# An earlier start for each scan direction's preparation, and a skewed first norm, in a four-layer vision-scan kernel

## The chip, the cores and the metric

The kernel runs on one core of a Trainium2 chip, in float32 throughout. The metric is device time in microseconds (us) for the whole program. Five engines work side by side, each through its own list of instructions in a fixed order: TensorE (PE, matrix products into PSUM), VectorE (DVE), ScalarE (ACT), GpSimd (POOL) and SyncE (SP), which here only issues data transfers (DMAs).

## The reference

Four layers follow each other on an image of shape (4, 96, 64, 64). Layers 0 and 2 are two-layer selective scans with a batch norm at the end, layer 3 is a depthwise 7x7 convolution with an MLP. The change is in layer 1, a state-space model in its chunked form (SSD), applied along four directions of each image:

```python
xn = rmsnorm(x, norm_w)                       # over the 96 channels
xs = [xn, flip(xn), transpose(xn), flip(transpose(xn))]   # 4 directions, 4096 tokens each
z, xBC, dt = split(xs @ in_proj_w.T)          # 192 | 192+128+128 | 3 heads
dt  = softplus(dt + dt_bias)
xBC = silu(conv_b + causal_conv4(xBC))
xh, Bm, Cm = split(xBC);  A = -exp(A_log)
# in chunks of tokens, with dAc = cumsum(dt * A):
y  = (Cm Bm^T * exp(dAc_s - dAc_t) * dt) @ xh + exp(dAc) * (Cm @ state)
y  = (y + D * xh) * silu(z)
y  = rmsnorm(y, gnorm_w) @ out_proj_w.T
out = mean over the 4 directions, each put back in place, + x
```

`x` of layer 1 is the result of layer 0: its batch norm's scale and shift applied to the raw output, plus layer 0's input.

## The kernel before

`program` (L1223) runs `mamba_fusion` (layer 0), `ssd` (layer 1), `mamba_fusion` (layer 2) and `convnext` (layer 3) one after the other. `mamba_fusion` leaves its output un-normed in DRAM (`raw`) and hands on scale and shift (`norm`); the next block applies them as it loads.

**How SSD is tiled.** A chunk is Q = 128 tokens, a block BLK = 1024 tokens or eight chunks. `run` (L986) lists 64 steps (b, o, r, blk): batch b of 4, orientation o (0 as it is, 1 transposed), r (0 forwards, 1 backwards), and 4 blocks. So 16 steps make a batch, and every fourth step begins a direction. The 512 chunks go through one loop with lags: `sums_to` (loads `dr`), `decay` (`seg`), `weights` (`cb`, `seg`, `xs`), `outputs` (`y`, state `prev`, `yz`, and at L931 its square sum on ACT), `scale`, `by_channels`, `finish` (adds into `X`, an SBUF image of the batch).

**The front of a block** (L780) is made while the block before it is worked on: `z` (PE L796, for r = 0 only), the two halves of the convolution (PE L814 and L825 from the stacked shifted copies `pk`), their additions (ACT L819, DVE L830), the silu (ACT L112) and transposes (L842). It is a generator, of which each point of the loop takes one step (two for the first block of an orientation), and it is finished at the block's last chunk.

**The preparation of a direction** is `prelude` (L763), also a generator. For r = 0 and o = 0 it begins with `rmsnorm` (L666): for each of NT = 8 pieces of 512 tokens, load `raw` and the residual, apply scale and shift (ACT L673), add (DVE L674), write the sum to DRAM (`src`), square (ACT L677), mean over channels (PE L679), inverse root (ACT L107, twice), and the product into `xn[0]` (DVE L682). For o = 1 it begins with `turn` (L685), eight transposing copies on POOL. Then `step_sizes` (L696): eight rows of dt (PE L706, ACT L711, a DMA to DRAM, L712), one load in another layout (`dtx`, L717), a softplus (L719 on), a transpose (L725). Last come `decays` (L729): PE L743, L745, L756, and a DMA of `rows`, from which `dr` is loaded. For r = 1 only `decays` is left. The loop takes one step of the preparation per chunk, and the rest at once at a fixed chunk:

```python
if n >= 0 and preludes and n // QB >= preludes[0][0] - 3:
    if n == (preludes[0][0] - 1) * QB - 1:
        for _ in preludes.pop(0)[1]:
            pass
```

So for a direction whose first step is N, the steps begin with block N - 3 and the rest is taken at the last chunk of block N - 2, before the front of step N begins.

**Start of SSD.** Two pieces of the norm, then all weights (`weights_of`, L616), then the rest of the first preparation, then `switch(0)` (L975: `X` loaded from `src`), then the whole first front, then the loop.

**What sets the order.** The code issues operations in program order; a scheduler then places them on the engines, and moves an operation ahead where its operands and buffers are free. Buffers come from pools, and a tile's buffer is taken over in program order: the tag "front" has two PSUM banks, which the preparation's products share with the fronts. All DMAs are issued by SP. Each transfer has one of a few semaphores in turn, and waits until the transfer that had it last is done.

Of the kernel before, what the change touches and what calls it, by code (L numbers as in the profile page):

```python
# [18 lines left out]
F32 = mybir.dt.float32  # L19
AF = mybir.ActivationFunctionType  # L20
ALU = mybir.AluOpType
# [4 lines left out]
B, C, HH, WW = 4, 96, 64, 64  # L26
# [546 lines left out]
class Ssd:  # L573
# [42 lines left out]
    def weights_of(self, w):  # L616

        nc, k, one = self.nc, self.k, self.one
        self.inw = one.tile([C + 1, 2 * DI + 2 * DST + NH], F32, name="inw")
        nc.sync.dma_start(self.inw, w["in"])  # L620

        conv = self.work.tile([P, 3 * BLK], F32, tag="pk", name="conv")
        conv = conv[:C, : 4 * CONV].rearrange("c (k n) -> c k n", k=4)
        nc.sync.dma_start(conv, w["conv_wT"].partition_broadcast(C))
        xbc = self.inw[:C, DI : DI + CONV]
        nc.vector.tensor_tensor(conv, conv, xbc[:, None].to_broadcast([C, 4, CONV]), ALU.mult)
# [12 lines left out]
        self.a = one.tile([P, 1, NH], F32, name="a")  # L639
        k.act.exp_ln(self.a[:, 0], self.ad[:, 0], AF.Exp)  # L640
        nc.vector.tensor_scalar_mul(self.a, self.a, -1.0)

        self.opw = one.tile([P, 4, C], F32, name="opw")
        gn = one.tile([P, 4], F32, name="gn")
        nc.vector.memset(self.opw, 0.0)
        nc.vector.memset(gn, 0.0)  # L650
        low, up = slice(0, HD), slice(HD, P)
        for j, rows, n, of in (
            (0, slice(0, P), slice(0, P), 0), (1, low, low, 1), (2, up, low, 0), (3, low, up, 0),
            (3, up, up, 2),
        ):
            nc.sync.dma_start(self.opw[rows, j], w["out"][n, of])
            nc.sync.dma_start(gn[rows, j : j + 1], w["gnorm"][n, of : of + 1])
        for j in range(4):
            nc.vector.tensor_scalar(
                self.opw[:, j], self.opw[:, j], gn[:, j : j + 1], 0.25, ALU.mult, ALU.mult  # L660
            )

    def bank(self, tag):
        return self.psum.tile([P, T], F32, tag=tag, name=tag, bufs=2)

    def rmsnorm(self, b):  # L666
        nc, k = self.nc, self.k
        for c in range(NT):
            t = ds(c * T, T)
            x, res = (self.work.tile([C, T], F32, name=n) for n in ("nx", "nr"))  # L670
            nc.sync.dma_start(x, self.raw[b, :, t])
            nc.sync.dma_start(res, self.res[b, :, t])
            nc.scalar.activation(x, x, AF.Identity, bias=self.bn[1], scale=self.bn[0])  # L673
            nc.vector.tensor_tensor(x, x, res, ALU.add)  # L674
            nc.sync.dma_start(self.src[b, :, t], x)
            sq = self.work.tile([C, T], F32, name="nsq")
            nc.scalar.activation(sq, x, AF.Square)  # L677
            pv = self.bank("front")[:C]
            nc.tensor.matmul(pv, lhsT=k.mean, rhs=sq, start=True, stop=True)  # L679
            rsqrt(k.act, sq, pv, self.eps)  # L680
            xn = self.xn[0][:C, ds(PAD + c * T, T)]
            nc.vector.scalar_tensor_tensor(xn, x, self.norm, sq, ALU.mult, ALU.mult)  # L682
            yield

    def turn(self):  # L685
# [7 lines left out]
            )  # L693
            yield

    def step_sizes(self, o):  # L696

        nc, k = self.nc, self.k
        n = NQ * NH
        rows = self.dram.tile([NH, L], F32, name="dtrows")
        for c in range(NT):
            pd = self.bank("front")[:NH]
            nc.tensor.matmul(  # L706
                pd, lhsT=self.inw[:, DI + CONV :], rhs=self.xn[o][:, ds(PAD + c * T, T)],
                start=True, stop=True,
            )
            row = self.work.tile([C, T], F32, tag="nsq", name="dtrow")[:NH]  # L710
            nc.scalar.copy(row, pd)  # L711
            nc.sync.dma_start(rows[:, ds(c * T, T)], row)  # L712
            yield
        x, ua, lg = (
            self.work.tile([n, Q], F32, tag=m, name=m, bufs=1) for m in ("dtx", "ua", "row")
        )
        nc.sync.dma_start(x, rows.rearrange("h (c t) -> c h t", t=Q))  # L717
        yield
        nc.scalar.activation(ua, x, AF.Abs)  # L719
# [43 lines left out]
    def prelude(self, b, o, r):  # L763

        if r == 0:
            yield from self.rmsnorm(b) if o == 0 else self.turn()
            yield from self.step_sizes(o)
        self.seq[b, o, r] = self.decays(r)

    def stack(self, o, r, blk):  # L770
# [9 lines left out]
    def front(self, b, o, r, blk, made, following):  # L780
# [205 lines left out]
    def run(self):  # L986
# [16 lines left out]
        def front(n):  # L1003
            if n >= len(steps):
                return iter(())
            return self.front(*steps[n], made[n], steps[n + 1] if n + 1 < len(steps) else None)
# [3 lines left out]
            (n, self.prelude(*steps[n][:3])) for n in range(0, len(steps), nblk)  # L1010
        ]
        first = preludes.pop(0)[1]
        for _ in range(2):
            next(first)
        self.weights_of(self.w)
        for _ in first:
            pass
        self.switch(0)
        for _ in front(0):
            pass  # L1020
        for n in range(-4, len(chunks) + 4):
            def at(lag):
# [289 lines left out]
```

## Time and profile before

| | us |
|---|---|
| median of 8 runs | 10003.18 (9988.59 to 10021.0) |
| profiled execution, own time | 10021.0 |
| its span, first to last instruction | 10019.0 |
| busy PE / DVE / POOL / ACT | 8622.6 / 8167.7 / 6975.5 / 5529.7 |
| norm's scale of layer 0 ready (end of DVE L561) | 3075 |
| first and last chunk's square sum (ACT L931) | 3191.8 and 6251.8 |
| moved by DMA | 1528.27 MB |

In the profile, busy time is that of executing instructions; PEld is the load of weights into PE, and lies beside PE's products. A row of the timeline gives the start, the length, the engine, the line, what is written from what, how many instructions were merged, and in brackets how long the engine had been idle and which engine or DMA ended that. SPq is SP's queue. The granted clock is that of PE, 1 being full speed.

### The profile page before, as it was taken

Reading aid. Unit: us, or ns where it says so; the run is one execution under the profiler, and the core shown is the slowest. Engines: PE = TensorE matmul, PEld = TensorE weight load, DVE = VectorE, ACT = ScalarE, POOL = GpSimd, SP = SyncE. Lnnn points to the kernel's source line nnn. Section 1 sums busy time; section 2 is a strip of 40 time slices with the busy share of each in tenths; the row PEclk is TensorE's granted clock in tenths of the full one; section 3 lists DMA queues with packets and bytes.
Section 4 is the critical chain, followed back from the end, with each engine's and each line's share of the span. In section 5 each row is a group of like instructions: output and inputs, shape, how many; then the busy total and the mean of one; then the engine's idle time right before and its main releaser. Section 6 shows DMA issues by size and latency. Waiting matters only on the chain. (4 is left out here: it accounts for less than half of the span.)

```text
span 10019.0 us, 109739 instructions
## 1 busy us (share of the span) xinstructions
PE 8622.6 (86%) x32744; PEld 3567.1 (36%) x32744; DVE 8167.7 (82%) x10861; ACT 5529.7 (55%) x10500; POOL 6975.5 (70%) x4600
## 2 busy tenths in 40 slices
PE   7888888888886988988898888788888888888688
PEld 1222222222213676676776777122221122221122
DVE  7999999999984666666766667799999999999787
ACT  5566666656653445545545544566666665665244
POOL 6888888888884555555555555688888888888322
PEclk9999999999987999999999999899999999998798
DMA  7677777667763223222322221767777777776442
GB/s 191 199 206 205 201 204 206 197 196 209 202 196 113 70 68 92 70 64 82 87 62 73 86 64 50 190 198 205 206 200 206 207 203 199 207 203 198 112 100 73
DMA packets 803534, 1528.27 MB, mean 153 GB/s; under 512 B 124253, under 2 KB 128249, under 8 KB 802170
## 3 DMA queue, kind: packets, MB, share of 16 engines
q1 hardware_dynamic: 802938, 1521.25, 53.6%
q8 instruction: 260, 4.26, 0.2%
q14 instruction: 336, 2.75, 0.1%
HBM read 1229.69 MB, written 156.37 MB: 138 GB/s over the span
## 5 line engine op out<-in xcount | busy, mean ns | idle before, releaser
L342 POOL TENSOR_TENSOR hc<-hs,bc 128x1024 f32<-128x1024 f32 x1536 | 3610.7, 2357 | 648.1 <-DVE hs L340 577.5
L340 DVE TENSOR_TENSOR_SCAN hs<-da,carry,bs 128x512 f32<-128x512 f32 x2016 | 2466.8, 1265 | 79.7 <-DVE bs L335 1.9
L107 ACT ACTIVATE da<-da,w_a 128x512 f32<-128x512 f32 x2304 | 1614.5, 715 | 1244.1 <-DMA da<-dd 1193.8
L361 PE MATMUL py<-hc,selsum 128*32 128x512 f32 x6144 | 1806.1, 640 | 469.6 <-POOL hc L342 459.3
L313 PE MATMUL bs<-du,seldu 64*128 64x512 f32 x4608 | 1589.0, 682 | 205.4 <-DVE hs L340 191.7
L335 DVE TENSOR_TENSOR bs<-bs,bc 128x1024 f32<-128x1024 f32 x1152 | 1398.5, 1214 | 196.8 <-PE bs L313 193.1
L308 POOL TENSOR_TENSOR du<-du,bc 128x1024 f32<-128x1024 f32 x384 | 905.1, 2357 | 273.1 <-DMA du<-dg 166.7
L361 PEld LDWEIGHTS py<-hc,selsum 128*32 128x32 f32 x6144 | 239.1, 110 | 1816.0 <-POOL hc L342 1113.5
L313 PEld LDWEIGHTS bs<-du,seldu 64*128 64x128 f32 x4608 | 451.7, 197 | 1208.2 <-DVE hs L340 850.1
L879 POOL TENSOR_TENSOR seg<-seg,cb 128x384 f32<-128x384 f32 x512 | 515.5, 1008 | 509.4 <-DVE cb L878 389.4
L194 PE MATMUL pu<-h,w_conv 96*128 96x512 f32 (+3 forms) x2048 | 832.7, 627 | 6.0 <-ACT rs L107 6.0
L863 DVE TENSOR_SCALAR seg<-dr,dac 128x128 f32<-128x128 f32 x1536 | 620.3, 436 | 261.5 <-PE y L908 244.5
L340 DVE TENSOR_TENSOR_SCAN hs<-bs,carry,du 128x512 f32<-128x512 f32 x672 | 823.5, 1260 | 6.5 <-issue 4.5
L814 PE MATMUL front<-pk,sconv 128*128 128x512 f32 x1536 | 746.3, 605 | 10.8 <-ACT z L802 7.0
L883 POOL TENSOR_TENSOR xs<-pre,coef 128x576 f32<-128x576 f32 x512 | 598.2, 1174 | 204.3 <-PE halves L922 148.6
L918 POOL TENSOR_TENSOR y<-y,xs 128x192 f32<-128x192 f32 x496 | 294.5, 594 | 545.5 <-DVE y L917 542.9
L931 ACT ACTIVATE y<-yz 128x192 f32<-128x192 f32 x512 | 186.1, 363 | 862.8 <-DVE yz L930 861.9
L825 PE MATMUL front<-sconv,pk 128*128 128x192 f32 x3072 | 572.8, 330 | 51.6 <-DVE pre L830 44.2
L1175 DVE SCALAR_TENSOR_TENSOR acc<-pad,c_conv,acc 96x1024 f32<-96x1024 f32 x336 | 491.5, 1467 | 110.2 <-ACT acc L1166 58.9
L345 ACT COPY carry<-hs 128x2 f32<-128x2 f32 x1344 | 251.1, 187 | 575.6 <-DVE hs L340 571.9
L825 PEld LDWEIGHTS front<-sconv,pk 128*128 128x128 f32 x3072 | 497.7, 190 | 82.4 <-DVE pre L830 70.2
L107 ACT ACTIVATE bs<-da,w_a 128x512 f32<-128x512 f32 x768 | 522.1, 680 | 3.4 <-DVE hs L340 1.4
(196 smaller groups left out, 13974.0 us busy)
## 6 DMA issues: line engine op xcount, KB each, us to landing
da<-dd SPq DMA_DIRECT2D x3072, 256.0 KB
du<-dg SPq DMA_DIRECT2D x768, 256.0 KB
dr<-rows SPq DMA_DIRECT2D x256, 384.0 KB
bc<-rows SPq DMA_DIRECT2D x256, 256.0 KB
dd<-delta SPq DMA_DIRECT2D x192, 256.0 KB
dg<-du SPq DMA_DIRECT2D x192, 256.0 KB
pk<-xn SPq DMA_DIRECT2D x128, 384.0 KB
pk<-xn SPq DMA_DIRECT2D x128, 256.0 KB
```

Of the source, the lines that this page charges most:

```text
L107: self.last = self.scalar.activation(out, in_, func, **kw)
L194: nc.tensor.matmul(pu[r0:r1], lhsT=wt["conv"][:kk, tap, d0:d1], rhs=h[:kk, b, ds(tap, T)], start=(tap == 0), stop=(tap == 3),)
L308: nc.gpsimd.tensor_tensor(g["du"], g["du"], self.b_or_c(g, 0), ALU.mult)
L313: nc.tensor.matmul(g["bs"][:, i], lhsT=self.sel["du"][rows, g["half"], g["q"]], rhs=g["made"]["du"][rows, g["j"]], start=True, stop=True,)
L335: nc.vector.tensor_tensor(dbx, dbx, self.b_or_c(g, 0), ALU.mult)
L340: nc.vector.tensor_tensor_scan(hs[:, i], da[:, i], dbx[:, i], init, ALU.mult, ALU.add)
L342: nc.gpsimd.tensor_tensor(g["hc"], hs, self.b_or_c(g, 1), ALU.mult)
L361: nc.tensor.matmul(py[rows], lhsT=self.sel["sum"][:, g["q"]], rhs=g["hc"][:, i], start=(g["q"] == 0), stop=(g["q"] == NQU - 1),)
L814: nc.tensor.matmul(p, lhsT=self.conv[:, i, DI + q * DST : DI + (q + 1) * DST], rhs=pk[:, i, ds(c * T, T)], start=(i == 0), stop=(i == 2),)
L825: nc.tensor.matmul(p, lhsT=pk[:, i, ds(c * Q, Q)], rhs=self.conv[:, i, :DI], start=(i == 0), stop=(i == 2),)
L863: nc.vector.tensor_scalar(seg[:, h], g["pair"]["dr"][:, c % 2 * NH + h], made["dac"][:, n0 + h : n0 + h + 1], 0.0, ALU.subtract, ALU.min,)
L883: nc.gpsimd.tensor_tensor(xs, x.to_broadcast([P, 3, NH, HD]), coef.to_broadcast([P, 3, NH, HD]), ALU.mult)
```

## The change

Three things are edited.

1. In the loop the preparation's steps begin one block earlier (`- 4` for `- 3`).
2. The first batch's norm is a new function, `begin`. All pieces are loaded at once, `raw` into `X` and the residual into `xn[1]`; the sum stays in `X`, so neither `src` nor the reload is needed for batch 0. The pieces go through in stages of which each is one piece behind the one before it, down to the dt rows. The weights are loaded in three parts, by a generator, and the first front is issued in between the steps of the preparation (one step after every third of the front).
3. In `rmsnorm` of the other batches each piece is loaded one step ahead of its use, which makes nine steps of eight. The write to `src`, and the dt rows' write to DRAM for all directions, are issued from ACT's queue instead of SP's.

```diff
@@ weights_of
         nc.sync.dma_start(conv, w["conv_wT"].partition_broadcast(C))
+        yield
         xbc = self.inw[:C, DI : DI + CONV]
...
         nc.vector.tensor_scalar_mul(self.a, self.a, -1.0)
+        yield
...
+    def begin(self):
+        nc, k = self.nc, self.k
+        rest = self.xn[1][:C]
+        for c in range(NT):
+            nc.sync.dma_start(self.X[:, ds(c * T, T)], self.raw[0, :, ds(c * T, T)])
+            nc.sync.dma_start(rest[:, ds(PAD + c * T, T)], self.res[0, :, ds(c * T, T)])
+            if c == 1:
+                yield
+        self.batch = 0
+        rows = self.dram.tile([NH, L], F32, name="dtrows")
+        sq, pd = {}, {}
+        for n in range(NT + 4):
+            if 0 <= (c := n - 4):
+                row = self.work.tile([C, T], F32, tag="nsq", name="dtrow")[:NH]
+                nc.scalar.copy(row, pd.pop(c))
+                nc.scalar.dma_start(rows[:, ds(c * T, T)], row)
+            if n < NT:
+                x = self.X[:, ds(n * T, T)]
+                nc.scalar.activation(x, x, AF.Identity, bias=self.bn[1], scale=self.bn[0])
+                nc.vector.tensor_tensor(x, x, rest[:, ds(PAD + n * T, T)], ALU.add)
+                sq[n] = self.work.tile([C, T], F32, tag=("nx", "nr")[n % 2], name="sq")
+                nc.scalar.activation(sq[n], x, AF.Square)
+            if 0 <= (c := n - 1) < NT:
+                pv = self.bank("front")[:C]
+                nc.tensor.matmul(pv, lhsT=k.mean, rhs=sq[c], start=True, stop=True)
+                rsqrt(k.act, sq[c], pv, self.eps)
+            if 0 <= (c := n - 2) < NT:
+                xn = self.xn[0][:C, ds(PAD + c * T, T)]
+                nc.vector.scalar_tensor_tensor(
+                    xn, self.X[:, ds(c * T, T)], self.norm, sq.pop(c), ALU.mult, ALU.mult
+                )
+            if 0 <= (c := n - 3) < NT:
+                pd[c] = self.step_rows(0, c)
+        return rows
+
     def rmsnorm(self, b):
...
+        loaded = []
+        for c in range(NT + 1):
+            if loaded:
+                n, x, res = loaded.pop()
+                nc.scalar.activation(x, x, AF.Identity, bias=self.bn[1], scale=self.bn[0])
+                nc.vector.tensor_tensor(x, x, res, ALU.add)
+                sq = self.work.tile([C, T], F32, name="nsq")
+                nc.scalar.activation(sq, x, AF.Square)
+                nc.scalar.dma_start(self.src[b, :, ds(n * T, T)], x)
...
+            if c < NT:
+                x, res = (self.work.tile([C, T], F32, name=n) for n in ("nx", "nr"))
+                nc.sync.dma_start(x, self.raw[b, :, ds(c * T, T)])
+                nc.sync.dma_start(res, self.res[b, :, ds(c * T, T)])
+                loaded.append((c, x, res))
             yield
...
+    def step_rows(self, o, c):
+        pd = self.bank("front")[:NH]
+        self.nc.tensor.matmul(
+            pd, lhsT=self.inw[:, DI + CONV :], rhs=self.xn[o][:, ds(PAD + c * T, T)],
+            start=True, stop=True,
+        )
+        return pd
+
-    def step_sizes(self, o):
+    def step_sizes(self, o, rows=None):
...
-            nc.scalar.copy(row, pd)
-            nc.sync.dma_start(rows[:, ds(c * T, T)], row)
-            yield
+        if rows is None:
+            rows = self.dram.tile([NH, L], F32, name="dtrows")
+            for c in range(NT):
+                row = self.work.tile([C, T], F32, tag="nsq", name="dtrow")[:NH]
+                nc.scalar.copy(row, self.step_rows(o, c))
+                nc.scalar.dma_start(rows[:, ds(c * T, T)], row)
+                yield
...
     def prelude(self, b, o, r):
         if r == 0:
-            yield from self.rmsnorm(b) if o == 0 else self.turn()
-            yield from self.step_sizes(o)
+            if (b, o) == (0, 0):
+                rows = yield from self.begin()
+                yield
+            else:
+                rows = None
+                yield from self.rmsnorm(b) if o == 0 else self.turn()
+            yield from self.step_sizes(o, rows)
         self.seq[b, o, r] = self.decays(r)
...
     def front(self, b, o, r, blk, made, following):
-        made.update(self.seq[b, o, r])
+        made.update(self.seq.get((b, o, r), {}))
...
     def run(self):
-        for _ in range(2):
-            next(first)
-        self.weights_of(self.w)
+        weights = self.weights_of(self.w)
+        next(first)
+        next(weights)
+        next(first)
+        next(weights)
+        for m, _ in enumerate(front(0)):
+            if m % 3 == 2:
+                next(first, None)
         for _ in first:
             pass
-        self.switch(0)
-        for _ in front(0):
+        made[0].update(self.seq[steps[0][:3]])
+        for _ in weights:
             pass
...
-            if n >= 0 and preludes and n // QB >= preludes[0][0] - 3:
+            if n >= 0 and preludes and n // QB >= preludes[0][0] - 4:
```

More of the change, by code (lines that the diff above doesn't have):

```diff
@@ L666, in rmsnorm @@
     def rmsnorm(self, b):
         nc, k = self.nc, self.k
[L668 to L682, printed above, removed]
+        loaded = []
@@ new lines, in rmsnorm @@
+        for c in range(NT + 1):
[6 more added lines that the diff above has]
+                nc.scalar.dma_start(self.src[b, :, ds(n * T, T)], x)
+                pv = self.bank("front")[:C]
+                nc.tensor.matmul(pv, lhsT=k.mean, rhs=sq, start=True, stop=True)
+                rsqrt(k.act, sq, pv, self.eps)
+                xn = self.xn[0][:C, ds(PAD + n * T, T)]
+                nc.vector.scalar_tensor_tensor(xn, x, self.norm, sq, ALU.mult, ALU.mult)
+            if c < NT:
[3 more added lines that the diff above has]
+                loaded.append((c, x, res))
@@ L694, in turn @@
             yield
-    def step_sizes(self, o):
+    def step_rows(self, o, c):
[6 more added lines that the diff above has]
+    def step_sizes(self, o, rows=None):
         nc, k = self.nc, self.k
         n = NQ * NH
[L703 to L710, printed above, removed]
-            nc.scalar.copy(row, pd)
-            nc.sync.dma_start(rows[:, ds(c * T, T)], row)
-            yield
+        if rows is None:
[5 more added lines that the diff above has]
+                yield
         x, ua, lg = (
```

## The prediction

> **What bounds the kernel now.** I read the page first, for which engine leads and where.
>
> ```profile
> span 10019.0 us, 109739 instructions
> PE 8622.6 (86%) x32744; PEld 3567.1 (36%) x32744; DVE 8167.7 (82%) x10861; ACT 5529.7 (55%) x10500; POOL 6975.5 (70%) x4600
> ```
>
> The change touches only the SSD stage, so everything is read there. It runs from 3075 us (the batch norm's scale is done at 3074.96) to 6257 us (last addition to X, L973). The 512 instructions of ACT L931, eight to a block of 1024 tokens, date its 64 blocks: the first at 3191.8, the last at 6251.8. So 116.8 us pass before the first, and the blocks take the rest. Their lengths from that list: 42 to 48 us for most, but four blocks before each new image orientation are long. For batch 0, blocks 4 to 7 take 44.0, 44.2, 54.9 and 57.5 (200.6 us); blocks 12 to 15, ahead of the next batch, 44.8, 56.9, 56.3 and 57.7 (215.7).
>
> Then the busy time by window: the start-up, blocks 4 to 7, and block 8 (columns: length, PE, PEld, DVE, ACT, POOL, granted clock, DMA share, GB/s).
>
> ```profile
> 3075.00:3192.00 117.00, 58.68 (x168) 29.68 (x168) 28.39 (x74) 45.25 (x71) 24.09 (x22) 0.67 0.50 146
> 3373.00:3416.00 43.00, 39.11 (x221) 31.31 (x220) 30.62 (x78) 21.27 (x50) 24.91 (x31) 0.96 0.25 74
> 3416.00:3461.00 45.00, 40.70 (x218) 31.29 (x218) 32.42 (x83) 21.20 (x51) 26.25 (x33) 0.92 0.25 71
> 3461.00:3516.00 55.00, 50.60 (x252) 34.98 (x252) 30.83 (x81) 24.80 (x57) 27.76 (x34) 0.91 0.16 46
> 3516.00:3573.00 57.00, 48.94 (x240) 40.19 (x240) 27.18 (x84) 26.97 (x62) 23.45 (x29) 0.85 0.21 64
> 3573.00:3621.00 48.00, 42.39 (x240) 34.30 (x239) 34.41 (x93) 24.43 (x59) 27.81 (x35) 0.96 0.25 75
> ```
>
> In a plain block PE is busy nine tenths: PE is the bound, and added PE work costs its length. The start-up is different, with no engine above 50%: a chain of waits. Block 7 has 8.1 us of idle PE and a clock of 0.85.
>
> The timeline shows why. First the start-up:
>
> ```profile
> 3095.31 2.02 DVE L626 TENSOR_TENSOR conv<-conv,inw 96x1792 f32<-96x1792 f32 x1 [9.17 <-DMA conv<-in_L_conv_wT]
> 3105.73 0.53 SPq L671 DMA_DIRECT2D nx<-raw  x1
> 3108.76 0.81 ACT L673 ACTIVATE nx<-nx,bn 96x512 f32<-96x512 f32 x1 [12.16 <-DMA nx<-raw]
> 3147.20 0.58 SPq L717 DMA_DIRECT2D dtx<-dtrows  x1
> 3149.78 0.31 ACT L719 ACTIVATE ua<-dtx 96x128 f32<-96x128 f32 x1 [4.20 <-DMA dtx<-dtrows]
> ```
>
> SP sits behind the weights' copies, so the third of eight pieces is loaded 30 us after the first. Then block 7:
>
> ```profile
> 3508.71 0.57 SPq L717 DMA_DIRECT2D dtx<-dtrows  x1
> 3518.39 0.29 ACT L719 ACTIVATE ua<-dtx 96x128 f32<-96x128 f32 x1
> 3528.33 3.04 PE L796 MATMUL front<-inw,xn 96*128 96x192 f32 x16
> 3531.29 10.57 PE L814 MATMUL front<-pk,sconv 128*128 128x512 f32 x24
> 3541.70 8.03 PE L825 MATMUL front<-sconv,pk 128*128 128x192 f32 x48
> 3554.74 1.09 PE L842 MATMUL front<-ident,pre 128*128 128x128 f32 x8 [2.98 <-ACT pre L112]
> ```
>
> The preparation is flushed at the end of block 6. Its last products hold the two "front" banks until 3527, so the whole front of block 8 comes in one lump of 21.4 us late in block 7, with PE waiting around it (ACT's silu).
>
> **What the Trainium skill says.** "DMA: Bandwidth & Descriptors", Anatomy of one DMA: a transfer has a fixed cost near 2.0 us besides its bytes. Here dtx, 48 KB, is read 2.6 us after its issue: agrees. The same page, Issuing engines are not separate DMA queues: another issuing engine saves only sequencer time. No run so far shows a DMA issued from ACT; SP's x<-nx issues take 0.30 us, dtrows 0.26. "Perfetto Trace Analysis", DMA Instruction HWDGE: the issuing sequencer itself waits for the semaphores before it is free; SP's queue above behaves so. "TensorE: Matmul & The Clock Gate", What's actually happening: idle stretches halve the array's clock. The 0.85 of block 7 and the 0.67 of the start-up agree.
>
> **The change part by part.** In the order in which the built instructions stand on each engine: before, the first orientation change has its decays at chunk 60 and the next front wholly behind them at chunk 61. After, the decays stand at chunk 50 and that front is spread over chunks 55 to 59. So the change does what it says.
>
> *Start-up.* Twelve transfers go (eight copies of x, four reloads of X: 3 MB); the sixteen piece loads are issued at once, ahead of the weights' dependent copies. Step by step, as estimates from the rows:
> - 18 issues of about 0.43 us from 3075.8. Their bytes (16 x 192 KB, inw 244 KB, conv 672 KB) are 4.1 MB; at 206 GB/s, the page's busy slices, 19.8 us, so the last lands near 3097. DVE's product of conv waits for 1.7 MB, 8.4 us and 2 us fixed, ends near 3088.5, and holds the third piece until then.
> - ACT per piece: 0.81 + 0.63 + 0.68 + 0.63 + 0.57 (row copy) + 0.30 (issue) = 3.6 us, eight times 29 us, 5.5 of it done by 3088. So 3112, and 3 us for the skewed stages: 3115 (3145 before).
> - Row landing to dtx read, 4.2 us before: 3119. Softplus to decays, 5.9 before, plus 3 between the front's groups: 3128. Decay rows to the first seg, 8.4 before: 3136.5.
> - The front meanwhile: z 4.9, conv 10.6 plus 2.1 of decays, to 3132. Its last 8.0 us need DVE's additions, which stand behind seg: to 3144.
> - Ahead of the silu ACT has the next batch's first piece, whose load SP issues behind six dr loads, and a copy out of it that waits for DVE. Behind these are the silu, hence PE's transposes and all chunks. I take 5 us: 3149. Silu to first L931, 12.4 before: 3162, against 3191.8. Gain 30 us. Bounds: 15 (DMA or the 5 us twice as bad) to 42 (no such holds).
>
> *Orientation changes* (four). Block 4 stays 44.0: the eight POOL copies lie under PE. The eight rows, 10.7 us over a plain block, move from block 6 to 5: 54.9. Block 6 keeps 44.2 plus the decays' PE work (0.42 + 0.58 + 0.69 + 0.42 = 2.1) and 1 us of wait: 47.3. Block 7 becomes a block that makes a front with z, 46.7 (mean of blocks 8 to 10), plus 1.7 for the reverse direction's decays: 48.4. Sum 194.6, against 200.6: 6 us, in all 24. Bounds for all: 0 to 30.
>
> *Batch changes* (three). Sums before 215.7, 216.7, 219.1: mean 217.2. After: block 12 takes the eight norms (12.5), 57; block 13 the rows in the tangle that block 14 shows now, 55; block 14 keeps two rows (2.7), decays (2.1), and 3 for its last conv products, which stand in one lump behind the decays: 52; block 15 48.4. Sum 212.4: 4.8 us, in all 14. Bounds: -10 (the norm, a block earlier, disturbs more) to 33 (all stalls gone: 206 each).
>
> *Copies moved to ACT.* Of 88 issues, 80 are in the steady part: 0.3 us each, 24 us of ACT. I cost them at nothing: ACT is busy 21 to 27 us of each 44 to 57. Without that cover they cost 24. Each also waits until an earlier transfer that used its semaphore has landed; behind it on ACT stand the exponentials of seg and the evacuations of front banks, for which POOL and PE wait. Before, these waits were SP's, which fed only loads issued early. Eight transfers stand between, usually over 10 us of this stage, so I take 0.
>
> Sum: 30 + 24 + 14 = 68 us. Against the profiled execution (10021 us, span 10019) that gives 9953. That execution was the slowest of the eight; against their median, 10003, it gives 9935.
>
> **Rivals.**
> 1. Only the start-up gains. PE is the bound in every block, and every product of the preparation remains, only elsewhere; the rows' 10.7 us speak for it. Against it: block 7's 8.1 us of idle PE and low clock. 10003 - 30 = 9973.
> 2. All stalls go. Start-up 40, orientation changes to plain work (three blocks of 44.2, one of 46.7, rows 10.7, decays 3: 193, thus 30 in all), batch changes to 206 (12.5 more for the norm; 33 in all): 9900. Against it: the lumps that remain in blocks 13 and 14 of the new order.
> 3. Slower: ACT becomes the place where DMA waits are served. If each of the 80 issues holds ACT, and PE behind it, for t, the gain is gone at 68/80 = 0.85 us, and it is slower beyond 0.2% at 1.1 us. At 2 us it gives 10003 - 68 + 160 = 10095. For it: ACT's order is fixed, and an SP load it waits for can itself be late (dr waits up to 15 us). Against: the distance of eight transfers, and ACT's idle half.
>
> **How the numbers follow.** Likeliest case 0.60 (own range 9915 to 9955); only the start-up 0.17; all stalls 0.13; slower 0.07; gains and losses cancelling 0.03. Predicted 9935. The range, 9890 to 9985, takes in the second and third case with their bounds and leaves out the slow one and most of the cancelling one. About 0.2%, 20 us, is what a measurement of this kernel can tell from no change. Faster by more: 0.60 + 0.13 + 0.15 of the start-up case = 0.88. Within: 0.05. Slower: 0.07.
>
> **What would show it.** First L931 near 3162 (the stage's start being the same); blocks 7, 23, 39 and 55 near 48 us with a clock over 0.9 and no 21 us lump; blocks 5 and its like near 55; block 12 near 57. Wrong would be: ACT idle for DMA ahead of its row copies or x copies, blocks 5 or 12 above 60, or a silu of the first front that waits long for nx.

## The result

The changed kernel takes 9935.5 us (median of 11 runs, 9914.2 to 9946.0) beside 10009.4 for the kernel before in the same comparison: a ratio of 0.9929, 95% interval 0.9919 to 0.9940, so about 71 us less. All differences below are worked out in this way: the ratio's distance from one, times the median of the kernel before that ran beside it.

The first lines of the page of the kernel after, span and busy time by engine:

```profile
span 9936.8 us, 109594 instructions
PE 8582.2 (86%) x32744; PEld 3521.3 (35%) x32744; DVE 8210.0 (83%) x10861; ACT 5529.3 (56%) x10500; POOL 6977.6 (70%) x4600
```

PE has the same 32744 products and is busy 40 us less. The change took no product from it; the same products last less, in line with a mean granted clock over the execution of 0.935 beside 0.930.

The stage's start (end of DVE L561) is at 3059.4 us here, against 3075.1 before; layer 0 is untouched, and over all executions below this lies between 3054 and 3087. So all places in the stage are counted from that point. L931 of before is L985 now. The busy time by window, for the start-up and then blocks 4 to 8 (columns: length, PE, PEld, DVE, ACT, POOL, clock, DMA share, GB/s):

```profile
3059.00:3157.00 98.00, 67.26 (x175) 31.33 (x175) 29.21 (x79) 43.90 (x73) 24.69 (x23) 0.64 0.48 138
3337.00:3380.00 43.00, 39.42 (x217) 31.57 (x216) 30.36 (x79) 20.77 (x50) 24.43 (x30) 0.92 0.24 74
3380.00:3435.00 55.00, 51.49 (x244) 33.49 (x243) 33.35 (x84) 25.11 (x58) 27.31 (x35) 0.94 0.21 60
3435.00:3483.00 48.00, 42.61 (x239) 34.92 (x237) 34.41 (x90) 24.92 (x63) 27.16 (x35) 0.93 0.22 68
3483.00:3527.00 44.00, 37.82 (x224) 30.64 (x224) 26.49 (x73) 22.96 (x54) 22.01 (x27) 1.00 0.22 64
3527.00:3576.00 49.00, 44.49 (x252) 36.31 (x250) 34.92 (x95) 24.98 (x57) 28.15 (x35) 0.97 0.24 73
```

Block 7 is now 44 us at a clock of 1.00 (57 at 0.85 before). The orientation's dt rows, now made in block 5, make that block ten us longer (53.9 on average beside 43.9). In sum over the stage, from the list of all 512 instructions of that line, the profiled executions differ so:

| part of the SSD stage | before | after | difference | prediction |
|---|---|---|---|---|
| start to the first L931/L985 | 116.7 | 97.4 | -19.3 | -30 |
| blocks 4 to 7 of each batch (4 groups) | 798.1 | 759.0 | -39.1 | -24 |
| blocks 12 to 15 (3 groups) | 651.4 | 638.7 | -12.7 | -14 |
| all other blocks | 1610.5 | 1603.9 | -6.6 | 0 |
| stage | 3176.7 | 3099.0 | -77.7 | -68 |

The time came out as forecast, but two of the four terms did not: the start-up gave a third less, the orientation changes 15 us more. The timeline of the new start-up shows the first:

```profile
3062.13 0.42 SPq L624 DMA_DIRECT2D conv<-in_L_conv_wT  x1
3069.97 1.02 SPq L675 DMA_DIRECT2D xn<-in_x  x1
3077.33 0.31 SPq L674 DMA_DIRECT2D X<-raw  x1
3079.06 2.02 DVE L627 TENSOR_TENSOR conv<-conv,inw 96x1792 f32<-96x1792 f32 x1 [9.45 <-DMA conv<-in_L_conv_wT]
3079.55 0.81 ACT L688 ACTIVATE X<-X,bn 96x512 f32<-96x512 f32 x1 [9.37 <-DMA X<-raw]
3113.97 0.58 SPq L766 DMA_DIRECT2D dtx<-dtrows  x1
3120.72 0.30 ACT L768 ACTIVATE ua<-dtx 96x128 f32<-96x128 f32 x1
```

The third piece reaches ACT 20.1 us after the stage's start, not 13.4, and dtx is used 6.75 us after its load's issue. And block 6, with the decays, and the front of block 8 in block 7, on PE:

```profile
3446.51 0.27 PE L805 MATMUL front<-ident,dac 128*96 128x128 f32 x1
...
3480.60 2.74 PE L868 MATMUL front<-pk,sconv 128*128 128x512 f32 x6
3484.04 2.84 PE L868 MATMUL front<-pk,sconv 128*128 128x512 f32 x6 [0.70 <-ACT z L856]
3488.04 1.88 PE L868 MATMUL front<-pk,sconv 128*128 128x512 f32 x4
```

The decays are through 36 us before block 7 begins (3482.8), and the front is cut into small portions with chunks between.

### The profile page after: what moved, and what is told of

Read it like the earlier page. It is cut to its first block, busy times and chain, and to the rows that moved or that the text cites. A ratio compares the mean times of both kernels' runs of the same rounds, so it can differ in the third digit from the quotient of the medians.

```text
span 9936.8 us, 109594 instructions
## 1 busy us (share of the span) xinstructions
PE 8582.2 (86%) x32744; PEld 3521.3 (35%) x32744; DVE 8210.0 (83%) x10861; ACT 5529.3 (56%) x10500; POOL 6977.6 (70%) x4600
## 5 line engine op out<-in xcount | busy, mean ns | idle before, releaser
L985 ACT ACTIVATE y<-yz 128x192 f32<-128x192 f32 x512 | 186.1, 363 | 907.8 <-DVE yz L984 907.0
L1235 DVE SCALAR_TENSOR_TENSOR acc<-pad,c_conv,acc 96x1024 f32<-96x1024 f32 x336 | 491.9, 1468 | 110.8 <-ACT acc L1226 59.9
```

Source lines behind the costliest of these rows:

```text
L1235: nc.vector.scalar_tensor_tensor(acc, images[b % 2][:, y : y + rows, x : x + WW], wt["conv"][:, tap : tap + 1], acc, ALU.mult, ALU.add,)
```

## The experiments

Where a kernel is called "early" or "late", that is when a preparation begins: with the first block of the direction ahead (as changed) or the second (as before). The flush is the rest of a preparation, taken at once at its fixed chunk. The orientation groups are blocks 4 to 7 of each batch, the batch groups blocks 12 to 15 of the first three. Sums of the stage's parts are from one profiled execution each. Groups of 16 blocks that no edit touches (blocks 0 to 3, and 8 to 11, of all four batches) lie between 721 and 737 us in all these executions, so a sum's difference under some 16 us says little by itself.

### Which part carries the gain

One edit to the kernel before:

```diff
-            if n >= 0 and preludes and n // QB >= preludes[0][0] - 3:
+            if n >= 0 and preludes and n // QB >= preludes[0][0] - 4:
```

> The kernel before with one edit: a preparation begins a block earlier. The start-up, the order inside the norm and the queue of the small copies stay as they were. By the prediction's steps: 24 us at the orientation changes and 14 at the batch changes, so 38 us below the kernel before. By the comparison of the two traces (39 us at the orientation changes, 13 at the batch changes, some 7 in the other blocks): 52 to 58 below. The rival in which only the start-up gains: no difference from before. First L931 of the stage at the same distance from the stage's start as before, about 117 us.

Measured: ratio 0.9926 (0.9909 to 0.9942), 74 us less. The start-up stays at 118.2 us; the orientation groups fall by 52 us to 745.9, the batch groups by 16 to 635.7. The rival in which only the start-up gains falls. But this one line alone gives as much as the whole change, so the rest of the change is worth nothing net, or parts of it cancel.

The reverse edit, made to the changed kernel (`- 4` back to `- 3`):

> The changed kernel with one edit undone: a preparation begins as late as before. What is left of the change is the new start-up, the norm in two skewed halves and the small copies on ACT's queue. By the prediction's steps: 30 us below the kernel before. By the comparison of the two traces: 19 to 25 below. The rival in which only the start-up gains: all of the 71 us. The long blocks ahead of an orientation change (blocks 7, 23, 39, 55) come back near 57 us, with their 21 us lump of the next block's front.

Measured: ratio 1.0016 (1.0006 to 1.0027), 16 us *more* than before, which no theory had. The start-up gained its 19.2 us, but the orientation groups are 9 us longer than before and the batch groups 23 us longer. So something in the rest of the change costs, more so when the beginning is late. Two candidates: the copies on ACT's queue and the skewed norm. The next run takes the first away, by giving the three `nc.scalar.dma_start` of small copies back to `nc.sync`:

> The run with the late beginning again (preparations as late as before, new start-up, skewed norm), but with the small copies back on SP's queue. With the copies on ACT that run was 19 us above the kernel before, its start-up 19 us shorter and its blocks 31 us longer. If the copies on ACT's queue are what lengthens the blocks, this run is 20 to 30 us below the kernel before, with the orientation and batch changes as before within 10 us. If it is the skewed norm, it stays within 10 us of the kernel before and the blocks ahead of a batch change stay 20 us longer in sum.

Measured: ratio 1.0003 (0.9996 to 1.0011), no difference that can be measured; start-up 91.9 us. The orientation groups come back to 793.4 (798.1 before), so there it was the copies, as far as so small a sum tells. The batch groups do not: 681.7, 30 us above before. There it is the norm's skew, the one thing left that touches them. The next two runs show by what means.

### What makes block 7 long

The prediction read from the trace that the late decays keep the two front banks and force the next front into one lump, and that the lump costs. This kernel is the changed one with the tail of each preparation left for the flush. The norm's nine steps and the eight rows (17), or the eight of the turn and the eight rows (16), are still taken one to a chunk:

```diff
-                else:
+                elif (steps[preludes[0][0]][2] == 0
+                      and n - (preludes[0][0] - 4) * QB < (17 if steps[preludes[0][0]][1] == 0 else 16)):
                     next(preludes[0][1], None)
```

> The changed kernel, in which each later preparation still starts a block earlier, but only its norm or turn and its rows are made early: the softplus, the decays and what follows wait until the last chunk of the block before last, where the kernel before made them. Theory: the late decays hold the two front banks and push the next block's front into a lump in block 7, and the 39 us at the orientation changes come from taking the decays away from there. Then blocks 7, 23, 39 and 55 go back to 55 to 58 us from 44.5, the preparations lose 10 us each, and of the 71 us some 15 to 35 are left. Rival: the gain comes from spreading the rows and the turn thinner; then the time is that of the changed kernel within 15 us.

Measured: ratio 0.9925 (0.9908 to 0.9943), 75 us less: nothing lost. In this kernel dtx's load and the first exponentials still come early, 48 and 43 us ahead of block 7; the decays come right at its start (3485.4). PE's timeline, with the decays' last product first:

```profile
3484.87 0.27 PE L805 MATMUL front<-ident,dac 128*96 128x128 f32 x1
...
3485.75 2.30 PE L850 MATMUL front<-inw,xn 96*128 96x192 f32 x12
...
3488.79 10.46 PE L868 MATMUL front<-pk,sconv 128*128 128x512 f32 x24
...
3502.03 6.01 PE L879 MATMUL front<-sconv,pk 128*128 128x192 f32 x36
```

The lump is there, 22 us of front with hardly a chunk between, as in the kernel before. But it begins with the block and not 13 us into it, and the block takes 45.0 us. So the lump by itself costs nothing; its lateness does.

Then it should not matter when a preparation begins, only when it ends. The kernel before with one edit:

```diff
                 else:
-                    next(preludes[0][1], None)
+                    for _ in range(2):
+                        next(preludes[0][1], None)
```

> The kernel before with one edit: a preparation still begins with the second block of the direction ahead, but takes two of its steps a chunk in place of one, so that it is through as early as in the changed kernel. Theory: block 7 is long because the chain of rows, dtx, softplus and decays ends some 13 us into it and the next front can't begin before; then only the end of the preparation counts, blocks 7, 15 and their like go to 45 to 47 us, and most of the gain is there, 45 to 75 us below the kernel before. Rival: beginning a block earlier gains because the preparation's work is spread thinner; then doubling it up in block 5 (13) costs what block 7 saves, and the time is within 20 us of the kernel before.

Measured: ratio 0.9928 (0.9913 to 0.9942), 72 us less, with a late beginning and the old start-up. Blocks 7 and 15 take 44.6 and 44.3 us on average. So what counts is when the preparation ends. The doubling up is not free before an orientation: block 6 takes 52.4 us there against 46.9 with the early beginning, and the orientation groups 770 us against 746. Before a batch it is better than free: 587 us against 636.

Over these runs the relation can be read off: the place of the decays' transposition on PE (L756, L805 in the changed kernel), from the block's start, against the length of that block (7, 15, 23, 31, 39, 47 and 55).

| kernel | decays, us from the block's start | length of the block, us |
|---|---|---|
| two steps a chunk, late | -40 to -35 | 44.3 to 45.4 |
| changed kernel | -37 to -31 | 44.5 to 45.5 |
| tail at the last chunk | -0.5 to 0.1 | 45.0 to 46.1 |
| before | 11.1 to 11.8 | 57.5 to 59.6 |
| late, skewed norm, copies on ACT | 13.6 to 14.6 | 59.9 to 61.0 |
| late, skewed norm, copies on SP: before an orientation | 11.0 to 11.7 | 57.8 to 59.2 |
| the same: before a batch | 16.0 to 16.3 | 63.8 to 64.4 |

From zero on, the block lasts the decays' delay and 45.5 to 48.3 us more: that is the time from the decays over the front to the next block's first sum. Before zero, being earlier buys one or two microseconds at most. This also explains the two runs with the late beginning. The skewed norm takes nine steps where the old one takes eight, so one more row waits for the flush; with the copies on SP the decays then come 4 to 5 us later, with those on ACT 2 us. Before an orientation the copies on ACT bring the decays to 14.4 us, from 11.1.

### The copies on ACT's queue

The changed kernel with L685, L716 and L761 issued by SP (`nc.scalar.dma_start` back to `nc.sync.dma_start`, three places):

> The changed kernel with the 88 copies that it gave to ACT's queue (L685, L716, L761) issued by SP again. The prediction costs the move at nothing: the same time as the changed kernel, within 10 us, so 61 to 81 below the kernel before. If the issues on ACT (0.24 to 0.50 us each in the changed kernel's trace, 80 in the steady part) lay on the path, 24 us would come back: 95 below. If instead it was the move that gave room to SP's loads, the gain shrinks to 50 or less, and SP's waits ahead of dr, nx and nr grow.

Measured: ratio 0.9891 (0.9875 to 0.9906), 109 us less than before and 38 less than the changed kernel; the two intervals lie apart. In the stage itself the two profiled executions differ by 20.6 us; the rest lies in layers that the edit doesn't touch. So I put the cost at 20 to 38 us, 0.23 to 0.43 us for each of the 88 copies. The prediction costed it at nothing. In the two kernels with the late beginning the same move is worth less: 1.0016 against 1.0003 is 13 us with intervals that overlap, and the stage differs by 5.5 us (start-up and orientation groups 19 us less on SP, batch groups 8 more).

Which blocks have it can be told over several runs. The start-up takes 97.1 to 97.5 us in the three runs with the copies on ACT and 91.9 to 94.3 in seven with them on SP. A part of that can be followed, in the changed kernel:

```profile
3141.47 0.81 ACT L712 ACTIVATE nx<-nx,bn 96x512 f32<-96x512 f32 x1 [8.08 <-DMA nx<-raw]
3142.31 0.69 DVE L713 TENSOR_TENSOR nx<-nx,nr 96x512 f32<-96x512 f32 x1 [2.36 <-ACT nx L712]
3142.92 0.35 DVE L884 TENSOR_TENSOR pre<-front,xbias 128x192 f32<-128x192 f32 x1
```

ACT waits 8.1 us for the next batch's first piece, DVE waits for ACT, and the front's last addition (L884) stands behind both. It begins 3.3 us after the addition before it, where the earlier ones are 1.0 us apart, and the silu needs it. With the copies on SP this piece comes to ACT at 3165.00, after the first L985 (3160.24): the edit changed the order that is built, and not only who issues. That is 2.4 us of about 5.

Block 12, with the norm's copies of x, takes 58.5 and 58.6 us on average in two runs with them on ACT and 54.0 to 54.9 in three with them on SP: about 12 us for three batches. Block 5, with the rows' copies, takes 53.7 and 53.9 us beside 51.8 to 53.7, which is hardly apart. In the three blocks 12 PE stands 10.3 us on average in the changed kernel and 8.3 with the copies on SP, and its products take 48.2 us beside 46.6, at a clock of 0.91 beside 0.93. A place where the two kernels differ, first in the changed one:

```profile
3749.78 0.88 PE L976 MATMUL halves<-xs,bt 128*128 128x192 f32 x2 [2.52 <-DVE cb L932]
3750.45 1.91 PE L718 MATMUL front<-nsq,mean 96*96 96x512 f32 x2
3752.16 1.38 PE L962 MATMUL y<-xs,seg 128*128 128x64 f32 x6
...
3764.67 1.05 PE L718 MATMUL front<-nsq,mean 96*96 96x512 f32 x2
```

And at the same place with the copies on SP:

```profile
3746.51 0.59 PE L976 MATMUL halves<-xs,bt 128*128 128x192 f32 x2 [1.27 <-DVE cb L932]
3746.93 1.02 PE L718 MATMUL front<-nsq,mean 96*96 96x512 f32 x2
3748.29 1.15 PE L962 MATMUL y<-xs,seg 128*128 128x64 f32 x6 [0.33 <-POOL seg L933]
...
3759.54 1.91 PE L718 MATMUL front<-nsq,mean 96*96 96x512 f32 x2
```

The norm's products for one piece take 1.91 us in one and 1.02 in the other, and PE waited 1.25 us longer just before. But for the next piece it is the other way about, 1.05 and 1.91: the stretches at half rate lie elsewhere, and one pair proves nothing. Of all 48 such products in the later batches, ten run at half rate in the changed kernel and five with the copies on SP. The issues themselves take 0.24 us of ACT for a row (56 in the steady part, median) and 0.36 for a piece of x (24), 22 us in sum, and ACT does not stand for a transfer in blocks 5 and 12 of batch 0. How the move comes to be a wait of PE in block 12, through ACT's order and DVE's, was not followed from link to link; that stays open.

### What bounds the new start-up

The changed kernel with the copies on SP, and the convolution weights' load issued behind the pieces of x:

```diff
+        yield
         conv = self.work.tile([P, 3 * BLK], F32, tag="pk", name="conv")
         conv = conv[:C, : 4 * CONV].rearrange("c (k n) -> c k n", k=4)
         nc.sync.dma_start(conv, w["conv_wT"].partition_broadcast(C))
-        yield
```

> The changed kernel with the small copies on SP's queue and the load of the convolution's weights issued behind the pieces of x in place of between them. The copies alone gave 111 us below the kernel before. In the changed kernel's trace the third piece waits 9.4 us on ACT, DVE's product of the weights waits 9.5 us for this load ahead of the piece's addition, and SP stands 6.3 us. If these waits bound the start-up, it goes from 92 to 80 to 86 us up to the first L931, and the run is 117 to 123 below the kernel before. If the tail of the start-up (rows, dtx, decays, silu) bounds it, it stays at 90 to 94 us; if the later sconv copies hold the convolution, it gets longer by up to 6.

Measured: ratio 0.9901 (0.9887 to 0.9915), start-up 94.2 us beside 92.3: no gain. The third piece still waits 9.85 us for its load. So it was not the 672 KB. What is slow then? The rate of the transfers in the changed kernel, from 3070 to 3080 us in 40 slices:

```profile
GB/s 334 215 117 143 307 240 84 141 266 283 94 21 31 21 31 21 31 21 31 21 31 21 21 31 21 31 21 39 29 29 29 29 29 115 205 361 131 25 25 74
```

For 5 us it is 21 to 39 GB/s, about a sixteenth of the 334 to 361 of its best slices, which fits one of the 16 DMA engines at work alone, and SP stands in that stretch. The Trainium skill has the reason ("DMA: Bandwidth & Descriptors", Why a DMA increments its semaphore by 16 and not by 1): a transfer is split over the largest number of engines up to 16 that divides the slowest dimension. The input weights have 97 rows, a prime: one engine carries all 243.6 KB. The test is to split them into 96 rows and one, here in the fastest kernel of the next section (copies on SP, the old norm for the later batches; start-up 93.6 us there):

```diff
-        nc.sync.dma_start(self.inw, w["in"])
+        nc.sync.dma_start(self.inw[:C], w["in"][:C])
+        nc.sync.dma_start(self.inw[C:], w["in"][C:])
```

> The fastest run so far (copies on SP, a batch's preparation in two steps a chunk, unskewed norm for the later batches) with the load of the input weights split: 96 rows in one transfer, the row of biases in another. In the start-up of the changed kernel the transfers fall from 181 GB/s to 17 to 34 GB/s from 3072.6 to 3077, one of 16 engines working alone, while SP stands and ACT waits 9.4 us for the third piece. Theory: it is the tail of this load, whose 97 rows are not spread over the engines. Then the third piece comes 5 to 8 us earlier, and the first L931 (L985) falls from 93.6 us after the stage's start to 86 to 90, if not the pace of the pieces behind it takes it back (then 92 to 94). The time: 132 to 140 us below the kernel before. Rival: the tail belongs to another transfer; then the slow stretch and the 93.6 us stay.

Measured: the first L985 (L981 there) 85.0 us after the stage's start, 8.6 earlier. The slow stretch is gone. The rate from 3054 to 3074 us, in 40 slices:

```profile
GB/s 0 33 1 0 0 20 184 332 283 225 263 194 298 250 269 269 229 238 236 195 244 231 242 266 279 275 279 283 250 283 275 262 266 270 266 266 274 268 215 145
```

Nor does ACT stand before the third piece:

```profile
3065.93 2.02 DVE L628 TENSOR_TENSOR conv<-conv,inw 96x1792 f32<-96x1792 f32 x1 [0.26 <-DMA conv<-in_L_conv_wT]
...
3066.81 0.80 ACT L689 ACTIVATE X<-X,bn 96x512 f32<-96x512 f32 x1
```

The stage starts at 3054.0 in this run, so the third piece comes at 12.9 us, where the prediction had 13.4 and the ten other runs with the new start-up have 17.2 to 21.2. It was the input weights' load, as the skill's rule says. As a time it is ratio 0.9859 (0.9839 to 0.9878), 141 us less; its interval overlaps that of the kernel without the split, so the gain is shown in the start-up and not in the sum.

### The batch changes

Block 13 takes 62 us in the changed kernel, at a clock of 0.83. The copies on SP, the conv load behind x as above, and three buffers for the pieces of the later norms (the rows' and the softplus's scratch tiles, and the squares of `begin`, move into these buffers too):

```diff
-                sq = self.work.tile([C, T], F32, name="nsq")
+                sq = res
...
-                x, res = (self.work.tile([C, T], F32, name=n) for n in ("nx", "nr"))
+                x, res = (self.work.tile([C, T], F32, name=n, bufs=3) for n in ("nx", "nr"))
```

> The run before this one (copies on SP, convolution's weights behind x), and the pieces of a later batch's norm have three buffers each in place of two, paid for by squaring into the buffer of the second summand. In the changed kernel block 13 takes 62 us at a clock of 0.83: the last piece of the norm is late because its load waits for a buffer. If that is the cause, blocks 12 and 13 fall from 117 together to about 105, and the run is 25 to 40 us below the run without it. If the loads wait for SP's place in its order (behind dr and pk) rather than for buffers, blocks 12 and 13 stay as they are.

Measured: ratio 0.9903 (0.9889 to 0.9917), blocks 12 and 13 at 54.9 and 62.0 us (54.0 and 64.4 without). Buffers are not the cause.

Two steps a chunk for all preparations had brought the batch groups to 587.0 us, 64 below before. Taken over into the kernel with the copies on SP, for the later batches alone:

```diff
+            batch = bool(preludes) and steps[preludes[0][0]][1:3] == (0, 0)
-            if n >= 0 and preludes and n // QB >= preludes[0][0] - 4:
+            if n >= 0 and preludes and n // QB >= preludes[0][0] - (3 if batch else 4):
...
                 else:
-                    next(preludes[0][1], None)
+                    for _ in range(2 if batch else 1):
+                        next(preludes[0][1], None)
```

> The changed kernel with the small copies on SP's queue, and a later batch's preparation (three of the seven) begun with the second block of the direction ahead and made in two steps a chunk, as the run with two steps a chunk did for all seven; an orientation's preparation begins with the first block and takes one step a chunk, as changed. In that run the blocks ahead of a batch change (12 to 15 and their like) took 587 us in sum against 622 with the early beginning. If the gains add, this run is 145 us below the kernel before (111 + 35), blocks 12 to 15 take 44, 60, 46 and 45 us. If the skewed norm, which has one step more and loads a piece a step ahead, doesn't bear two steps a chunk, block 13 goes above 65 and the run is 111 to 125 below.

Measured: ratio 0.9898 (0.9883 to 0.9913), 102 us less; block 13 takes 66.7 us and the batch groups 623.0. The gain did not come along. The same with the kernel before's norm (load and use of a piece in one step, eight steps) for the later batches:

> The run before this one with the kernel before's norm for the later batches, load and use of a piece in one step. If skewing the norm is worth anything, blocks 12 and 13 are longer here than there, by 5 us or more a batch and 15 in all; if not, the two runs are within 10 us and both near 145 below the kernel before.

Measured: ratio 0.9868 (0.9848 to 0.9889), 132 us less; the batch groups are 587.9 us. Block 13 of the first batch, in the run with the skewed norm:

```profile
3759.78:3828.70 68.92, 58.52 (x248) 36.96 (x248) 44.84 (x95) 40.91 (x81) 34.27 (x40) 0.88 0.34 104
```

and in the run with the old norm:

```profile
3743.30:3803.54 60.24, 54.04 (x251) 34.22 (x250) 42.64 (x95) 40.97 (x82) 36.62 (x40) 0.97 0.42 126
```

About as many products of PE, but 4.5 us less of its time for them, at a clock of 0.97 against 0.88. PE waits 5.1 us ahead of the norm's mean (L718) with the skewed norm and 1.1 us with the old one. Skewing a stage was meant to take waits away; here, with two steps a chunk, it has more of them. What in the built order does that is open.

The run with the skewed norm and two steps a chunk again, begun a block earlier:

> A later batch's preparation in two steps a chunk, but begun with the first block of the direction ahead, all else as in the first run of this set. It tells why the batch changes gained 64 us with two steps a chunk and 13 with one. If what counts is that norm and rows lie together in one block (one block disturbed in place of two), blocks 12 and 13 take 60 and 45 us, and the run is within 10 us of the first. If what counts is the place, block 13 in place of 12, it is 20 to 40 us slower than the first.

Measured: ratio 0.9884 (0.9863 to 0.9905), 116 us less; blocks 12 and 13 take 66.6 and 49.2 us. That is neither expectation, but it is not slower than with block 13, so the place is not what counts. With the skewed norm and the copies on SP the batch groups take 622 to 626 us early at one step a chunk, 623 late at two, 613 early at two; with the old norm 636 early at one and 587 to 590 late at two. The old norm early at two was not tried.

## Why the prediction was right, and where not

**The time.** 9935 was forecast and 9935.5 measured. That closeness is partly luck, as the steps show.

**Start-up: mis-sized, 30 us forecast, 19.3 measured.** The term that failed is the landing of the loads ("at 206 GB/s ... DVE's product of conv ... ends near 3088.5", that is 13.4 us after the start). It ended at 21.7 us. Nor was it DVE's product that held the third piece: ACT waited 9.4 us for the piece's own load, and still 9.9 us with the conv load moved behind. The prediction's own line from before was a warning: the conv load was issued at 3081.62 there and its product began at 3095.31, 13.7 us later, with less traffic around it, and the sum has 10.4 (8.4 and 2 fixed). The mean rate does not hold for a load that one engine carries. With the load split the product ended 14.0 us after the start, and the start-up (with the copies on SP, too) gained 31.7 us: the forecast's size. As for the 2 us fixed, the section of the Trainium skill that the prediction cites for them ("DMA: Bandwidth & Descriptors", Anatomy of one DMA) is about transfers that GpSimd issues, while SP issues these; 2.6 us from issue to use of dtx were measured in the old start-up, and 6.75 in the new one. Two more terms were low. From the third piece to the last row copy I had 26.5 us; it took 33.1 (31.2 with the split load). From the last row to dtx in use I had 4.2; it took 8.1 with the copies on ACT. On the other side, the front was not held by all of it: the silu comes 10 us later than forecast, where dtx is 17 us later. The piece of the next batch ahead of the silu, one of the prediction's signs of being wrong, did hold it, by 2.4 of the 5 us set aside.

**Orientation changes: mis-sized, 24 us forecast, 39 measured.** Blocks 5 and 6 are as forecast (54.9 and 47.3; measured on average 53.9 and 47.8). Block 7 is the term: 48.4 forecast, 44.8 measured, four times. I had priced it as a block that makes a front with z, at the clock of blocks 8 to 10. The first three of these blocks run at 1.00; but the fourth runs at 0.925 and takes 45.5 us beside their 44.5, so the clock is at most one of the 3.6 us, and what makes up the rest was not taken apart. The reason given was half right. That the flush at the end of block 6 is late, and that the front waits for it, is shown. That the lump itself is the cost is refuted: with the lump at the block's start the block is as short.

**Batch changes: 14 us forecast, 12.7 measured**, but not by the blocks given: 57, 55, 52, 48.4 forecast; 58.5, 62.3, 46.8, 45.3 measured on average. Blocks 14 and 15 gained more, as block 7 did, and block 13 was underpriced by 7 us. So the sum came right by errors that cancel, and a difference of 12.7 us in one execution says little by itself.

**Copies on ACT: forecast 0, cost 20 to 38 us.** The prediction named 24 us for the case that the cover is gone, and that is the size. "ACT is busy 21 to 27 us of each 44 to 57" was no cover; by which link the cost reaches PE is shown for a part of the start-up alone. That the issue would wait for earlier transfers, the mechanism of the third rival, does not show in blocks 5 and 12: the issues take 0.24 to 0.50 us each, and ACT's waits there are for PE and DVE.

**The rivals.** Only the start-up (9973): refuted, since the early beginning alone gives 74 us with the old start-up. The change without the early beginning gives nothing, but it has the skewed norm in it, which costs 30 us there; the new start-up quite by itself was not run. All stalls go (9900): not reached by the changed kernel, whose block 13 keeps its stall, as the prediction said; passed by the kernel with the copies on SP, the old norm and two steps a chunk for the batches (132 us less). Slower: its size per copy, 0.23 to 0.43 us, stayed below the break-even of 0.85.

**What the sum hid.** Start-up -19, blocks ahead of changes -52 and the rest -7 make up the stage. By the experiments the same total is the early beginning (-74), the new start-up without ACT's copies (-24), those copies (+20 to 38), and a skewed norm that costs nothing measurable with one early step a chunk and 30 us with the late beginning. That gives 60 to 78 us less, with 71 measured. An addition of independent parts would have been wrong: what the norm's skew and the copies cost depends on when the preparations begin.

## What to carry to other kernels

When a flush ends a prepared chain, find when its last result is there, measured from the point where it is first needed: past that point each microsecond cost about one here, before it an earlier result bought nothing, and a lump of work that came in time was free. An engine that is half idle is no cover for instructions put into its fixed order: 88 short ones, 24 us in sum, cost 20 to 38 here. A load's row count belongs in its price: take the engines that share it, not the mean rate.

## What was not expected of the hardware

A load of 97 rows (243.6 KB) let the transfers fall to 21 to 39 GB/s for 5 us and held the loads behind it; as 96 rows and one it did not, and the third piece came 12.9 us after the stage's start, not 20.8 as in the same kernel without the split. The same load is in the kernel before, with 26 GB/s on average from 3089.5 to 3092.5 us there.

PE's granted clock differs between kernels with the same products: block 7 goes from 0.85 to 1.00, and the norm's products run at half rate now here, now there. The Trainium skill says that idle stretches lower the clock ("TensorE: Matmul & The Clock Gate", What's actually happening). These runs agree only in part. With more waiting in block 12 came a lower clock (10.3 us and 0.91 beside 8.3 and 0.93), so there the wait is paid twice, once as idle time and once in slower products. But block 7 is idle for 14% of its time in both kernels, 8.1 of 57 us and 6.2 of 44, at 0.85 in one and 1.00 in the other: the idle share alone does not set the clock, and what does was not worked out.
